# Ten normalizations move from VectorE to GpSimd in the first stage of a decoder kernel

## The chip, the cores and the metric

The kernel runs on one core of a Trainium2 chip. The time is that of one execution on the device in microseconds (us); less is better. In all that follows PE is TensorE (matmuls and transposes), DVE is VectorE, ACT is ScalarE, POOL is GpSimd, and SP is the engine whose queue issues the DMAs.

## What is computed

The reference is a decoder of two layers, all float32, on x of shape (8, 128, 512) and a context of the same shape. After each of six blocks stands the sum with the block's input and a normalization over the last axis:

```python
def _layernorm(x, axis=-1, eps=1e-05):
    m = jnp.mean(x, axis=axis, keepdims=True)
    v = jnp.var(x, axis=axis, keepdims=True)
    return (x - m) / jnp.sqrt(v + eps)
...
x = _layernorm(x + _L0_attn_ref(x, ...))            # causal attention, 32 heads of 16
x = _layernorm(x + _L0_xattn_ref(x, ctx, ctx))      # autocorrelation: FFT, top 9 lags, softmax, shifted sums
x = _layernorm(x + _L0_ffn_ref(x, ...))             # 28 experts of rank 8, the best 2, beside a base matrix
x = _layernorm(x + _L1_attn_ref(x, ...))            # attention with ALiBi
x = _layernorm(x + _L1_xattn_ref(x, ctx, ...))      # attention to the context and itself
x = _layernorm(x + _L1_ffn_ref(x, ...))             # low-rank heads, weighted by a softmax
```

The change concerns the first two of these six normalizations.

## The kernel before

**Tiling.** Each of the 8 batch elements is one block of 128 tokens and so one tile of 128 partitions by 512 features. The program names them by block: x_in_b is the input of block b, x_a0_b the result after the first attention, x_c0_b that after the autocorrelation, x_f0_b after the experts. The profile leaves the numbers out, so x_a and x_c are these tiles (x_a also the ones of the second layer's attention).

**A normalization** is made by two helpers. `add_norm` adds the block's result, which lies in PSUM, to the old x on DVE (L103). `moments` then runs bn_stats (L91), bn_aggr (L93) and the addition of eps (L95) on DVE, which leaves the mean in the tile mv; POOL raises variance plus eps to the power −0.5 (L97), which gives the scale rs. Last, one tensor_scalar over 128x512 subtracts the mean and multiplies by the scale, in place (L107); before the change it runs on DVE. With the argument `later`, everything after the sum is put on a list (`late`) that `catch_up` works off in the next step.

**The first stage** has 16 steps: 4 pairs of blocks by 4 groups of 8 heads. In a step, `Heads16` makes scores in PSUM (L165), adds the mask (L369) and takes the maxima (L182) on DVE; ACT takes the exponentials (L194); a step later `turn` transposes them on PE (L225), with copies out of PSUM on DVE and ACT (L226) under the tile name pT_a, and takes the reciprocal of the sums (L215, rc_a), which POOL spreads over the features (L218, rb_a) for PE to transpose (L233, pr_a); after that `out` multiplies by the values (L244, L250; the result is scaled at L258, oT). Beside it, `queries_keys` prepares the next step (kbd on DVE, L358). The output projection of block b (po, L86) runs in the steps f = 1 and 2 of the next pair; its `add_norm` defers the normalization by a step.

**The autocorrelation** of a pair of blocks is cut into pieces, which the loop places into later steps (pairs 0 and 1) or after it (2 and 3): `spectra` multiplies the normalized x_a and the context with a table of waves on PE (L395: pa from x_a, pb from the context) and forms products (ACT's xa, L401; DVE's L405 and L407; POOL's L406 and L408); `correlate` (pc, L417; ACT's co, L422); `chosen` finds the best lags on DVE (L432 to L446) with help of POOL (L440, L447) and ACT; `shifted` (pvf L457, pw L461, ACT's wf L466, DVE's vw L469 and L471, POOL's L470 and L472); `done` makes poc (L86) and the `add_norm` into x_c. The experts' first reader of x_c transposes it (pt_xTf, L129).

**Order.** Each engine works off its own queue in order. A scheduler in the framework fixes these orders when the program is built, from the order of the calls and its own estimates; `issue_after` pins some of them. PSUM tiles come from two pools, four single banks and two pairs of banks. The scores, pT_a's transposes and pa, pb, pc, pvf and pw share the two pairs, so a matmul into a pair waits for whoever reads the pair's last content.

The stage on which the change bears lies between about 73 and 213 us of the span.

Of the kernel before, what the change touches and what calls it, by code (L numbers as in the profile page):

```python
# [13 lines left out]
ALU = mybir.AluOpType  # L14
# [4 lines left out]
B, S, D = 8, 128, 512  # L19
# [24 lines left out]
def decoder(ctx: ExitStack, tc: tile.TileContext, a: dict, out: bass.AP):  # L44
    nc = tc.nc
# [11 lines left out]
    def bank(name):  # L57
        return ps1.tile([P, 512], F32, tag="ps1", name=name)
# [24 lines left out]
    def mm_acc(ps, pairs):  # L83
        n = len(pairs)
        for i, (l, r) in enumerate(pairs):
            nc.tensor.matmul(ps, lhsT=l, rhs=r, start=(i == 0), stop=(i == n - 1))  # L86

    def moments(src, name):

        st = sm.tile([P, 6], F32, tag="bnst", name=f"st_{name}")  # L90
        nc.vector.bn_stats(st, src)  # L91
        mv = sm.tile([P, 2], F32, tag="bnmv", name=f"mv_{name}")
        nc.vector.bn_aggr(mv, st)  # L93
        ve = sm.tile([P, 1], F32, tag="ve", name=f"ve_{name}")
        moments.done = nc.vector.tensor_scalar(ve, mv[:, 1:2], EPS, None, ALU.add)  # L95
        rs = sm.tile([P, 1], F32, tag="rs", name=f"rs_{name}")
        nc.gpsimd.tensor_tensor(rs, ve, neghalf, ALU.pow)  # L97
        return mv[:, 0:1], rs

    def add_norm(x_old, ps, name, later=None):  # L100

        r = xp.tile([P, D], F32, tag="x", name=f"x_{name}")
        nc.vector.tensor_tensor(r, ps, x_old, ALU.add)  # L103

        def normalized():
            mean, rs = moments(r, name)
            return nc.vector.tensor_scalar(r, r, mean, rs, ALU.subtract, ALU.mult)  # L107

        if later is None:
            add_norm.done = normalized()  # L110
        else:
            later.append(normalized)
        return r

    late = []
# [162 lines left out]
    xs = [None] * B  # L278
# [92 lines left out]
    def projection(b, oT):  # L371
        po = bank(f"po0_{b}")
        mm_acc(po, [(oT[:, b % 2, c, :], wo[:, c, :]) for c in range(NC)])
        nc.gpsimd.tensor_tensor(xs[b], xs[b], bqkv[:, 1, :], ALU.add)
        xs[b] = add_norm(xs[b], po, f"a0_{b}", late)


    def swapped(t):
# [3 lines left out]
    class Correlated:  # L382
# [92 lines left out]
        def done(self, h):  # L475
            b = self.bs[h]
            po = bank(f"poc_{b}")
            mm_acc(po, [(dft[:, T_J + i * P : T_J + (i + 1) * P], self.ri[h][i]) for i in range(2)])
            xs[b] = add_norm(xs[b], po, f"c0_{b}")

        def pieces(self):

# [30 lines left out]
    for n, (p, f) in enumerate(steps):  # L513
# [23 lines left out]
        if 0 < f < 3 and p:  # L537
            projection(2 * p - 3 + f, oTs[p - 1])
# [15 lines left out]
    for j in range(2):  # L554
        projection(B - 2 + j, oTs[NP - 1])
# [56 lines left out]
    def shared_expert(b, xT, hs):  # L612
        po = bank(f"pof0_{b}")
        for c in range(NC):
            shared_expert.done = nc.tensor.matmul(po, lhsT=xT[:, c, :], rhs=wbase[:, c, :], start=(c == 0), stop=False)  # L615
        return hs, po
# [6 lines left out]
    def chosen_experts(b, hT, po, later=None):  # L623
        for j in range(2):
            chosen_experts.done = nc.tensor.matmul(
                po, lhsT=hT[:, j, :], rhs=wlb[:, j, :], start=False, stop=(j == 1)
            )
        xs[b] = add_norm(xs[b], po, f"f0_{b}", later)
# [104 lines left out]
    hs, po = shared_expert(0, *routes[0])  # L733
# [110 lines left out]
    for b in range(B):  # L844
# [3 lines left out]
        for f in (0, 2):  # L848
# [27 lines left out]
            now.divide(0, moments.done if f == 0 and b + 1 < B else None)  # L876
            now.exps(1)
            half = projection(b - 1, oT_before) if f == 2 and b else iter((0, 0))
            next(half)
            if b + 1 < B:  # L880
# [26 lines left out]
    with stage("x1b", 2, side="right") as ap, stage("f1", 2, side="right") as fp:  # L907
# [146 lines left out]
        def turned_heads(b, ls):  # L1054
            pt = bank(f"pt_lT_{b}")
            nc.tensor.transpose(pt[:, :P], ls.rearrange("p h r -> p (h r)"), ident)
            lT = fp.tile([P, P], F32, tag="lT", name=f"lT_{b}")

            nc.scalar.mul(lT, pt[:, :P], H1 * 32.0 / R1)
            return lT  # L1060

        def low_sum(b, lT):
            po = bank(f"pof1_{b}")
            nc.tensor.matmul(po, lhsT=lT, rhs=wb, start=True, stop=True)
            return po
# [12 lines left out]
        def low_scores(b):  # L1078
            scores_low[b] = scored(b, tokens_low.pop(b))

        def low_turn(b):
            turned_lows[b] = turned_heads(b, scores_low.pop(b))
# [87 lines left out]
        po = projection(B - 1, oTs_x.pop(B - 1), {3: [lambda: low_scores(B - 2)], 8: [lambda: low_turn(B - 2)]})  # L1170

        def summed(name, po, x_old):
            r = xp.tile([P, D], F32, tag="x", name=f"x_{name}")
            added = nc.vector.tensor_tensor(r, po, x_old, ALU.add)
            return r, added
# [5 lines left out]
        r, _ = summed("x1_last", po, xs[B - 1])  # L1181
        norm = moments(r, "x1_last")
        po = low_sum(B - 2, turned_lows[B - 2])
# [11 lines left out]
        r, _ = summed(f"f1_{B - 1}", low_sum(B - 1, turned_heads(B - 1, ls)), x_last)  # L1195
# [144 lines left out]
```

## Time and profile before

| | us |
|---|---|
| median of 3 runs | 883.65 |
| lowest and highest | 882.28 and 884.38 |
| the profiled execution | 884.56 |
| its span, first to last instruction | 882.8 |
| busy in the span: PE, DVE, ACT, POOL | 854.3, 565.3, 369.5, 190.3 |
| mean granted TensorE clock | 0.992 |

All rows shown below come from the one profiled execution. Its span is 1.8 us shorter than its own time. Matmuls are pipelined and their ends are modelled, so a busy PE is one that has a matmul under way and not one at its peak. Where a row ends with a bracket, it gives the idle time of the engine before the instruction and what ended it; a row of a group has the count, the busy time and the mean duration in ns; a row with three numbers and slashes has the shortest, median and longest duration in ns.

### The profile page before, as it was taken

How to read it: one execution, taken by the hardware profiler on the slowest of the kernel's cores; microseconds unless marked ns; L12 is line 12 of the kernel's file. 1: busy time of each engine (PE TensorE's matmuls, PEld its weight loads, DVE VectorE, ACT ScalarE, POOL GpSimd, SP SyncE). 2: the span in 40 equal slices, each digit the busy share in tenths (PEclk: the TensorE clock that was granted, in tenths of full speed). 3: DMA queues.
4: the chain of work that ended last, by engine and by line, in shares of the span. 5: the costliest groups of instructions: out<-in, count | busy, mean ns of one | idle time of the engine just before them, and what ended most of it. 6: DMA issues, size and time to landing. Idle time of an engine off the chain costs nothing.

```text
span 882.8 us, 16963 instructions
## 1 busy us (share of the span) xinstructions
PE 854.3 (97%) x6454; PEld 525.1 (59%) x6454; DVE 565.3 (64%) x1329; ACT 369.5 (42%) x1534; POOL 190.3 (22%) x267
## 2 busy tenths in 40 slices
PE   9999999999899999999999999999999999999996
PEld 5766655655445555555555687758475846576442
DVE  3756787786868657888888612725363545467653
ACT  3787465565222216666666603213122322224310
POOL 2500232232333224555555300000000000000000
PEclk9999999999999999999999999999999999999998
DMA  9700000130300002000003020332113211313330
GB/s 329 303 2 25 2 13 13 49 104 6 144 12 24 1 0 72 26 1 2 2 2 144 26 73 1 73 90 46 41 35 93 44 46 38 81 42 80 86 88 36
DMA packets 30066, 50.68 MB, mean 57 GB/s; under 512 B 5536, under 2 KB 22048, under 8 KB 28192
## 3 DMA queue, kind: packets, MB, share of 16 engines
q1 hardware_dynamic: 27424, 47.49, 18.1%
q10 hardware_dynamic: 2560, 2.10, 1.1%
q8 instruction: 51, 0.84, 0.4%
q14 instruction: 31, 0.25, 0.1%
HBM read 30.69 MB, written 2.10 MB: 37 GB/s over the span
## 4 chain that ended last, share of the span: by engine, by line
PE 63%; DVE 21%; ACT 11%; issue 2%; POOL 2%; DMA 1%; SPq 1%; ACTq 0%; POOLq 0%; DVEq 0%
PE pqx L86 9%; PE pox L991 8%; ACT e_a L194 8%; PE pkx L86 4%; PE pvx L86 4%; PE s_x L929 4%; PE o_x L974 4%; PE pq L86 3%; PE pk L86 3%; DVE e_a L715 3%; PE pv L86 3%; DVE m_a L182 2%; PE pof L615 2%; PE pt_a L225 2%; PE s_a L165 2%
## 5 line engine op out<-in xcount | busy, mean ns | idle before, releaser
L194 ACT ACTIVATE e_a<-e_a,m_a 128x128 f32<-128x128 f32 (+1 forms) x512 | 184.8, 364 | 94.3 <-DVE m_a L182 94.3
L950 ACT ACTIVATE e_x<-s_x,m_x 128x256 f32<-128x256 f32 x128 | 58.7, 484 | 139.3 <-DVE m_x L940 130.9
L194 ACT ACTIVATION_READ_ACCUMULATOR e_a<-e_a,m_a 128x1 f32 x512 | 97.0, 189 | 0.0
L991 PE MATMUL pox<-w_X_o,oTx 128*128 128x512 f32 x192 | 84.9, 596 | 0.7 <-DVE oTx L980 0.6
L86 PE MATMUL pqx<-xTx,w_X_q 128*128 128x256 f32 x384 | 84.9, 380 | 0.0
L86 PEld LDWEIGHTS pqx<-xTx,w_X_q 128*128 128x128 f32 x384 | 72.5, 190 | 11.4 <-issue 1.8
L939 DVE TENSOR_REDUCE m_x<-s_x 128x4 f32<-128x1024 f32 x32 | 37.6, 1218 | 41.1 <-PE s_x L929 41.1
L991 PEld LDWEIGHTS pox<-w_X_o,oTx 128*128 128x128 f32 x192 | 35.7, 190 | 46.0 <-issue 44.3
L182 DVE TENSOR_REDUCE m_a<-e_a 128x4 f32<-128x512 f32 (+1 forms) x128 | 62.7, 543 | 0.0
L97 POOL TENSOR_TENSOR rs_x<-ve_x,neghalf 128x1 f32<-128x1 f32 x7 | 3.9, 550 | 268.6 <-DVE ve_x L95 249.6
L208 POOL TENSOR_TENSOR e_a<-e_a,rc_a 128x512 f32<-128x512 f32 x64 | 52.7, 847 | 17.1 <-DVE rc_a L205 16.5
L225 PE MATMUL pt_a<-ident,e_a 128*128 128x128 f32 x384 | 48.6, 274 | 4.5 <-DVE e_a L369 3.9
L225 PEld LDWEIGHTS pt_a<-ident,e_a 128*128 128x128 f32 x384 | 43.5, 140 | 12.3 <-DVE e_a L369 4.9
L929 PE MATMUL s_x<-kTx,qTx 32*128 32x256 f32 x768 | 50.0, 385 | 0.7 <-ACT e_x L950 0.7
L929 PEld LDWEIGHTS s_x<-kTx,qTx 32*128 32x128 f32 x768 | 39.0, 184 | 16.8 <-issue 11.7
L974 PE MATMUL o_x<-pT_x,vx 128*32 128x512 f32 x384 | 43.7, 595 | 1.8 <-issue 0.6
L958 DVE STREAM_TRANSPOSE e_x<-e_x 128x1024 f32<-128x1024 f32 x32 | 39.7, 1241 | 0.8
L957 DVE TENSOR_SCALAR e_x<-e_x,rc_x 128x256 f32<-128x256 f32 x128 | 36.3, 347 | 3.9 <-DVE rc_x L954 2.6
L103 DVE TENSOR_TENSOR x_x<-pox,x_a 128x512 f32<-128x512 f32 x7 | 4.8, 686 | 52.5 <-PE pox L991 52.5
L165 PEld LDWEIGHTS s_a<-kbd,qT 32*64 32x64 f32 x1024 | 20.7, 131 | 28.4 <-issue 12.7
L835 ACT COPY qTx<-pqx 128x512 f32<-128x512 f32 x24 | 14.1, 594 | 55.5 <-PE pqx L86 55.2
L165 PE MATMUL s_a<-kbd,qT 32*64 32x256 f32 (+1 forms) x1024 | 33.2, 335 | 2.1 <-DVE pT_a L226 1.2
(223 smaller groups left out, 1618.0 us busy)
## 6 DMA issues: line engine op xcount, KB each, us to landing
pT_x<-e_x SPq DMA_DIRECT2D x224, 64.0 KB, 2.0
w_X_q<-in_X_q SPq DMA_DIRECT2D x3, 1024.0 KB, 4.9
w_X_o<-in_X_o SPq DMA_DIRECT2D x3, 1024.0 KB, 4.8
w_L_Wv<-in_L_Wv SPq DMA_DIRECT2D x2, 1024.0 KB, 6.7
w_L_Wo<-in_L_Wo SPq DMA_DIRECT2D x2, 1024.0 KB, 7.6
x_in<-in_x SPq DMA_DIRECT2D x8, 256.0 KB, 7.5
ct<-in_ctx SPq DMA_DIRECT2D x8, 256.0 KB, 2.8
cT<-in_ctxT SPq DMA_DIRECT2D x4, 512.0 KB, 3.8
```

The lines of the kernel that those rows point to most:

```text
L86: nc.tensor.matmul(ps, lhsT=l, rhs=r, start=(i == 0), stop=(i == n - 1))
L165: nc.tensor.matmul(s[r // 2][64 * u : 64 * u + 64, r % 2, cols], lhsT=qT[rows, 64 - 64 * part : P - 64 * part], rhs=kbd[rows, :, :keys], s ...
L182: self.scored = nc.vector.tensor_reduce(self.m[:, part, rs, :], self.by_heads(part)[:, rs], AX.X, ALU.max, negate=True)
L194: nc.scalar.activation(e[:, r, x, :], e[:, r, x, :], AF.Exp, bias=self.m[:, part, r, x : x + 1], accum_out=self.su[:, part, r, x : x + 1],)
L208: nc.gpsimd.tensor_tensor(e, e, bc(self.rc[:, part, rs, :].unsqueeze(3), list(e.shape)), ALU.mult)
L225: nc.tensor.transpose(pt[:, r, cols], self.e[:, 2 * i + r, cols], ident)
L929: nc.tensor.matmul(sc[g // 2][:, g % 2, u * 256 : (u + 1) * 256], lhsT=qT[rows, (h0 + u) * NS + n, :], rhs=kT[rows, n], start=(n == 0), st ...
L939: nc.vector.tensor_reduce(m, self.s[i], AX.X, ALU.max, negate=True)
L950: nc.scalar.activation(self.e[:, :, j, :], self.s[half][:, i, :].rearrange("p (a k) -> p a k", k=32), AF.Exp, bias=self.m[:, j : j + 1], s ...
L958: nc.vector.transpose(self.e[:, :, js, :], self.e[:, :, js, :])
L974: nc.tensor.matmul(po[32 * g : 32 * g + 32, :], lhsT=v[:, s, g * XD + 32 * n : g * XD + 32 * n + 32], rhs=pT[:, s].rearrange("p i h x -> p ...
L991: nc.tensor.matmul(po, lhsT=oT[:, n, h * P : (h + 1) * P], rhs=w, start=(i == 0), stop=(i == NX - 1))
```

## The change

`add_norm` takes the engine of the final tensor_scalar as an argument. For the first attention, blocks 0 to 5 pass GpSimd, and blocks 6 and 7 VectorE as before; for the autocorrelation, blocks 0 to 3 pass GpSimd, and 4 to 7 VectorE. These are ten instructions. Sums, moments and scales stay where they were. In the changed file the lines from 101 on have numbers that are higher by one.

```diff
-    def add_norm(x_old, ps, name, later=None):
+    def add_norm(x_old, ps, name, later=None, engine=nc.vector):
+
 
         r = xp.tile([P, D], F32, tag="x", name=f"x_{name}")
         nc.vector.tensor_tensor(r, ps, x_old, ALU.add)
 
         def normalized():
             mean, rs = moments(r, name)
-            return nc.vector.tensor_scalar(r, r, mean, rs, ALU.subtract, ALU.mult)
+            return engine.tensor_scalar(r, r, mean, rs, ALU.subtract, ALU.mult)
...
-        xs[b] = add_norm(xs[b], po, f"a0_{b}", late)
+        xs[b] = add_norm(xs[b], po, f"a0_{b}", late, nc.gpsimd if b < B - 2 else nc.vector)
...
-            xs[b] = add_norm(xs[b], po, f"c0_{b}")
+            xs[b] = add_norm(xs[b], po, f"c0_{b}", engine=nc.gpsimd if b < B // 2 else nc.vector)
```

## Prediction

> **What bounds the kernel now.** I read the page first: busy times and the chain.
>
> ```profile
> PE 854.3 (97%) x6454; PEld 525.1 (59%) x6454; DVE 565.3 (64%) x1329; ACT 369.5 (42%) x1534; POOL 190.3 (22%) x267
> PE 63%; DVE 21%; ACT 11%; issue 2%; POOL 2%; DMA 1%; SPq 1%; ACTq 0%; POOLq 0%; DVEq 0%
> ```
>
> PE is hardly ever without a matmul, so shorter DVE work pays only where PE stands still and the wait ends on DVE. The ten instructions that move lie between 73 and 213 us. So I then asked for PE's waits from 60 to 225 us, which answers in six lines:
>
> ```profile
> PE pt_a L225 <- DVE e_a L369: 3.9, 2, 2.0
> PE pa L395 <- DVE pT_a L226: 0.6, 1, 0.6
> PE o_a L244 <- DVE ve_a L95: 0.4, 1, 0.4
> PE pt_a L225 <- ACT e_a L194: 0.4, 1, 0.4
> PE pvf L457 <- ACT pT_a L226: 0.3, 1, 0.3
> PE s_a L165 <- DVE vw L471: 0.2, 1, 0.2
> ```
>
> Columns: total us, times, longest. All PE idling in the stage is 5.8 us. The 3.9 us are two waits behind the top-k work (110 to 112 and 174 to 176 us); no moved instruction runs near them. Only the second line has one on its path, as the chain from 72 to 92 us shows (start, us, what):
>
> ```profile
> 83.22 0.15 DVE ve_a L95
> 83.37 0.66 DVE kbd L358
> 84.03 0.01 issue
> 84.05 0.55 DVE x_a L107
> 84.59 0.88 DVE pT_a L226
> 85.47 0.04 issue
> 85.51 1.94 PE pa L395 x8
> ```
>
> x_a here is token block 1. The normalization stands on DVE ahead of the copy that frees the PSUM pair which pa wants; PE's previous matmuls ended at 84.87.
>
> **Removed from DVE.** Ten L107 instructions (x_a of blocks 0 to 5, x_c of 0 to 3). L107's view gives:
>
> ```profile
> L107 DVE TENSOR_SCALAR x_a<-x_a,mv_a,rs_a x16: 540/546/1418, 73.6 to 513.2; 128x512 f32<-128x512 f32 x16
> ```
>
> Ten times 0.546 is 5.5 us of DVE. In the built order of the changed program PE, ACT and SP keep their order, DVE loses the ten (and one bn_aggr passes an oT multiply), and on POOL each stands directly behind the L97 of its norm. What follows each on DVE decides:
>
> - x_a 0 (73.64): pT_a comes 0.5 earlier, then DVE idles 2.76 us for ACT's exps, with PE unbroken. Zero.
> - x_a 1 (84.05): pT_a starts at 84.03, pa at about 84.95 instead of 85.51. Gain 0.55. It holds downstream: s_a at 91.87 needs the PSUM pairs that DVE's L407 frees at 91.64; L405 ahead of it waits for ACT's xa (to 89.7, ACT busy throughout) and can move forward about 0.2, so s_a arrives at 91.3 and finds its second pair free at about 91.5, which it wants 0.2 later. I book 0.5.
> - x_a 2, 3, 4 (129.81, 145.96, 192.38): the next but one on DVE is L103 x_c, which waits 0.9 us for PE's poc. Zero each.
> - x_c 0, 2 (134.63, 197.21): DVE then idles 2.04 us for ACT's wf. Zero.
> - x_c 1 (151.50): DVE waits 0.88 us for rs_c, then goes on with L405, for which pb ends at 151.8; the following v waits 1.14 us for PE. Zero.
> - x_a 5, x_c 3 (209.25, 211.99): ACT's exps end the wait of pt_a at 211.71. Only pa at 212.19, which the trace shows 0.17 us behind DVE's pT_a on the weight load, can come earlier: 0 to 0.17; I take 0.1.
>
> Cover for the zeros is PE's own stream; were it gone, they would be worth at most 8 × 0.55 = 4.4 us.
>
> **Added on POOL.** No row shows a 128x512 tensor_scalar there. The nearest:
>
> ```profile
> L440 POOL TENSOR_TENSOR ex<-co,top 128x512 f32<-128x512 f32 x8 | 8.4, 1049 | 21.3 <-DVE top L432 21.2
> L408 POOL TENSOR_TENSOR pr<-pr 128x512 f32<-128x512 f32 x4 | 5.1, 1275 | 3.7 <-DVE mv_f L93 3.7
> L270 POOL MEMSET vd<- 128x512 f32 x6 | 3.4, 572 | 0.0
> ```
>
> A memset (writes only) 0.57, two full inputs 1.28, one full and one broadcast input 1.05. The last is nearest in shape: I take t = 1.05, ends 0.57 and 1.28. In all 10.5 us more POOL, which is at 22%.
>
> [...]
>
> Readers of the results. x_a 1 is the only tight one: rs ends at 84.00, t puts it ready at 85.1; pa reads block 0 first (two calls each of about 0.43 × 2 us, block 1 from 84.95 + 0.86 = 85.8). Slack 0.7, so it holds to t = 1.75. x_a 3 is ready at 147.0, read from 149.0. x_a 5 at 210.3, read from 213. x_c 0 to 3 are read by the transposes at 207.5, 210.1 and after 239; for 2 and 3 that is over 25 us.
>
> Queued behind each on POOL: after x_a 0, 1, 3 POOL idled 4.6 us, after x_a 2 and 4 4.3 us ahead of rs_c: absorbed. Behind x_c 0 and x_c 2 stands rb_a with only 0.3 us to spare, so it ends about 0.5 to 0.7 later; its reader, PE's pr_a, comes 8 us later or more. Behind x_c 1 comes L406, 1.8 us away. Behind x_a 5 and x_c 3: rs_c 3 (before at 211.08) starts by 210.7, x_c 3 ends near 212.3, rb_a near 212.7 (before 213.24; PE wants it at 213.36). Zero.
>
> **A shared port.** One of the DVE rows shows a clash: x_a at 224.28 took 1.42 us while POOL ran memsets until 226.2; that one (block 6) stays. The work beside the ten moved ones on DVE reads PSUM (pT_a, L103, L405) or is a bn_stats; the pT_a row is 906 to 958 ns in all 32 cases. I cost contention at zero, with up to 0.4 us at x_c 3 where a reciprocal (L215) may wait.
>
> [...]
>
> **Sum.** −0.5 − 0.1 = −0.6 us. The profiled execution took 884.56 (span 882.8 and 1.8 around it), 0.9 above the median 883.65: 884.0 for such an execution, **883.05** for the median. As bounds of the mechanism: −0.7 to +0.4 (gain lost and the reciprocal's wait).
>
> **What can blur it.** PE's granted clock falls in places after an idle stretch: it is 0.79 over 112 to 120 us.
>
> ```profile
> 113.88 2.08 PE L86 MATMUL po<-w_L_Wo,oT 128*128 128x512 f32 x2
> 115.75 2.54 PE L457 MATMUL pvf<-ct,dft 128*128 128x512 f32 x4
> ...
> 177.35 1.12 PE L86 MATMUL po<-w_L_Wo,oT 128*128 128x512 f32 x2
> 178.80 1.98 PE L457 MATMUL pvf<-ct,dft 128*128 128x512 f32 x4 [0.33 <-ACT pT_a L226]
> ```
>
> The same work 64 us later, behind an equal 1.96 us of idling, runs at full clock: one slow stretch costs (2.08 − 1.12) + (2.54 − 1.98) = 1.5 us, and it does not always come. The three times before span 2.1 us, so a median can shift by one.
>
> [...]
>
> **Rivals.**
> 1. *No change in kind (chance 0.50).* The sum above; 881.9 to 885.4.
> 2. *Faster (0.31).* The 0.6 and one slow stretch fewer: 883.65 − 0.6 − 1.5 = 881.5. For it: 0.55 us less idling and earlier phases in a stage with three idle stretches of 2 us. Or part of the covered 4.4 us becomes real, where PE's continuous busy time hides waits (s_a at 122.51 took 1.86 for 0.91). Against: those waits end on vw and ACT.
> 3. *Slower (0.19).* POOL's tensor_scalar with two per-partition operands is slow. From t = 1.75 pa waits for x_a 1. From t = 1.55 rb_a 3_3 (209.25 + t + 0.55 + t + 0.40, wanted at 213.3) holds pr_a, at 2 us for each us of t. At t = 2.5: 0.75 + 1.9 − 0.6 = +2.0, so 885.7. For it: L97's single column takes 0.55 us, far more than its one element explains. Against: every full-width row of POOL is under 1.3.
> 4. *The move does nothing on DVE* (the waits it removes were PE's anyway): 883.65, within case 1.
>
> **Chances.** 0.2% is 1.77 us, about what a measurement of this kernel can tell from no change. Faster by more needs −1.2 beyond my sum, slower +2.4. 0.31, 0.50 and 0.19. Range: from 883.65 − 0.7 − 1.5 − 0.5 (one slow stretch fewer and one of the eight covered instructions turned real) = 881.0 to 883.65 + 0.4 + 1.5 (one slow stretch more) = 885.5.
>
> **What would show it.** Right: pa's wait of 0.64 gone, x_a and x_c on POOL at about 1.05, DVE's busy time down by some 5.5, rb_a never ending a PE wait, PE's two waits of 2.0 unchanged. Wrong: a PE wait that ends on x_a or rb_a; POOL's L107 over 1.55; a gain over 1.2 at PE's unchanged clock.

## The result and the profile after

The changed kernel took 886.44 us (median of 8 runs, 884.56 to 887.34) against 883.91 for the kernel before in the same comparison (8 runs, 882.28 to 884.90): a ratio of 1.0027, interval 1.0016 to 1.0038. A second comparison, shown below as e12, gave 1.0029 (1.0019 to 1.0039). So the change costs 2.2 to 2.5 us; the forecast was a gain of 0.6. The profiled execution took 887.34 with a span of 885.6, 2.8 longer than the span before.

Line numbers are those of the changed file, one higher than before from 101 on. The page's busy times and the shares of the chain:

```profile
PE 855.7 (97%) x6454; PEld 526.1 (59%) x6454; DVE 560.7 (63%) x1319; ACT 369.5 (42%) x1534; POOL 210.1 (24%) x277
...
PE 61%; DVE 21%; ACT 12%; POOL 2%; issue 2%; DMA 1%; ACTq 0%; POOLq 0%; DVEq 0%; SPq 0%
```

DVE lost 4.6 us. That is less than ten times 0.546, because the rows of neighbouring instructions overlap in the profile (before, the row behind x_a 0 begins 0.47 us after it) and because one other instruction took 0.47 longer (the last section). POOL gained 19.8, where the forecast booked 10.5. POOL's rows, grouped by form, say why:

```profile
L108 POOL TENSOR_SCALAR x_a<-x_a,mv_a,rs_a 128x512 f32<-128x512 f32 x6 | 12.5, 2080 | 0.6
...
L108 POOL TENSOR_SCALAR x_c<-x_c,mv_c,rs_c 128x512 f32<-128x512 f32 x4 | 8.3, 2077 | 0.4
```

One of them takes 2.08 us, 3.8 times its 0.546 on DVE. PE's waits from 60 to 225 us (total us, times, longest) show where that reaches the engine that sets the end:

```profile
PE pt_a L226 <- DVE e_a L370: 3.9, 2, 2.0
PE pr_a L234 <- POOL rb_a L219: 1.0, 1, 1.0
PE o_a L245 <- DVE ve_a L95: 0.4, 1, 0.4
...
PE pa L396 <- POOL x_a L108: 0.2, 1, 0.2
```

The two long waits behind the top-k work are what they were. pa's wait of 0.64 on DVE's copy is gone, as the change meant it. Two new waits end on POOL, and both are of this change.

**The first place, at 84 us.** PE's timeline in the changed kernel:

```profile
84.40 1.02 PE L86 MATMUL pv<-w_L_Wv,xT 128*128 128x512 f32 x2
85.57 1.07 PE L396 MATMUL pa<-x_a,dft 128*64 128x512 f32 x2
86.88 1.50 PE L396 MATMUL pa<-x_a,dft 128*64 128x512 f32 x5 [0.24 <-POOL x_a L108]
...
90.46 1.12 PE L86 MATMUL pv<-w_L_Wv,xT 128*128 128x512 f32 x2
```

Before, pa started at 85.51, with no wait inside it, between these two rows:

```profile
83.85 1.02 PE L86 MATMUL pv<-w_L_Wv,xT 128*128 128x512 f32 x2
...
89.10 2.84 PE L86 MATMUL pv<-w_L_Wv,xT 128*128 128x512 f32 x6
```

From pv to pa 1.66 became 1.17 us, the gain of 0.5 that was forecast. From pa to pv 3.59 became 4.89, a loss of 1.3. Net +0.81, and this still holds behind the next matmuls (from pv to the first o_a 9.67 us, 8.85 before). The bracket shows only 0.24 of idling; the rest of the loss is hidden in PE's busy time, and the experiments explain it.

**The second place, at 213 us.** POOL's timeline, and PE's beside it:

```profile
210.21 0.56 POOL L97 TENSOR_TENSOR rs_a<-ve_a,neghalf 128x1 f32<-128x1 f32 x1 [5.04 <-DVE ve_a L95]
210.88 2.08 POOL L108 TENSOR_SCALAR x_a<-x_a,mv_a,rs_a 128x512 f32<-128x512 f32 x1
212.93 0.56 POOL L97 TENSOR_TENSOR rs_c<-ve_c,neghalf 128x1 f32<-128x1 f32 x1
213.60 2.08 POOL L108 TENSOR_SCALAR x_c<-x_c,mv_c,rs_c 128x512 f32<-128x512 f32 x1
215.62 0.40 POOL L219 COPY rb_a<-rc_a 128x256 f32<-128x256 f32 x1
```

```profile
214.74 0.33 PE L226 MATMUL pt_a<-ident,e_a 128*128 128x128 f32 x1
216.07 0.44 PE L234 MATMUL pr_a<-ident,rb_a 128*128 128x128 f32 x2 [1.01 <-POOL rb_a L219]
```

Before the change PE's two rows were these:

```profile
213.19 0.33 PE L225 MATMUL pt_a<-ident,e_a 128*128 128x128 f32 x1
213.36 0.38 PE L233 MATMUL pr_a<-ident,rb_a 128*128 128x128 f32 x2
```

POOL works without a gap from the scale of block 5 to rb_a; both long instructions stand ahead of a copy of 0.40 that PE wants. From the last pt_a to pr_a it was 0.17 us before (213.19 to 213.36) and is 1.33 here: +1.16.

0.81 and 1.16 make 2.0 of the 2.2 to 2.5 us. The two spans differ by 2.8: beside these 2.0, the start took 0.5 longer and x_a of block 6 another 0.5 (the last section for both), while the program's last two matmuls took 1.12 where they took 1.89, at a granted clock of 0.97 from 860 to 882 us where it was 0.84; some 0.5 us more is spread over the rest.

### The profile page after: what moved, and what is told of

Its sections match the earlier page's. It is cut to its first block, busy times and chain, and to the rows that moved or that the text cites. A ratio compares the mean times of both kernels' runs of the same rounds, so it can differ in the third digit from the quotient of the medians.

```text
span 885.6 us, 16973 instructions
## 1 busy us (share of the span) xinstructions
PE 855.7 (97%) x6454; PEld 526.1 (59%) x6454; DVE 560.7 (63%) x1319; ACT 369.5 (42%) x1534; POOL 210.1 (24%) x277
## 4 chain that ended last, share of the span: by engine, by line
PE 61%; DVE 21%; ACT 12%; POOL 2%; issue 2%; DMA 1%; ACTq 0%; POOLq 0%; DVEq 0%; SPq 0%
PE pqx L86 9%; ACT e_a L195 8%; PE pox L992 8%; PE pkx L86 4%; PE pvx L86 4%; PE s_x L930 4%; PE o_x L975 4%; PE pq L86 3%; DVE e_a L716 3%; DVE m_a L183 3%; PE pk L86 3%; PE pv L86 2%; PE pof L616 2%; PE pt_a L226 1%; PE po L86 1%
## 5 line engine op out<-in xcount | busy, mean ns | idle before, releaser
L97 POOL TENSOR_TENSOR rs_x<-ve_x,neghalf 128x1 f32<-128x1 f32 x7 | 3.8, 548 | 268.9 <-DVE ve_x L95 249.9
```

## The experiments

Two theories. **Late results:** a GpSimd instruction of 2.08 us costs only where somebody wants its result, or a result queued behind it, at once; that is at block 1 and at block 5 with x_c 3. **Toll:** each moved instruction costs some 0.25 us (the 2.5 of the change over ten), by a clash with VectorE or by later work on GpSimd. Each timed kernel is compared with the kernel before in runs on the same chip; differences are of medians. The brackets hold the ratio to the kernel before and its 95% interval; the ratio is estimated by itself and can differ from that of the medians by half a microsecond and more.

**Taking them back.** e1 puts block 1 of the attention back on VectorE, e2 block 3 of the autocorrelation, e3 both. Their edits are the conditions in the two calls, in e3:

```diff
-        xs[b] = add_norm(xs[b], po, f"a0_{b}", late, nc.gpsimd if b < B - 2 else nc.vector)
+        xs[b] = add_norm(xs[b], po, f"a0_{b}", late, nc.gpsimd if b in (0, 2, 3, 4, 5) else nc.vector)
...
-            xs[b] = add_norm(xs[b], po, f"c0_{b}", engine=nc.gpsimd if b < B // 2 else nc.vector)
+            xs[b] = add_norm(xs[b], po, f"c0_{b}", engine=nc.gpsimd if b < 3 else nc.vector)
```

> Undoes one of the ten: x_a of block 1 is normalized on DVE again, nine stay on POOL. Theory (two late results: x_a 1 for pa, worth +0.8 us net, and rb_a behind x_a 5 and x_c 3, worth +1.2; another 0.5 in a DVE row of 1.89 us at x_a 6): pa waits 0.6 us for DVE's pT_a as before the change, rb_a still ends a PE wait of 1.0; the time is 0.8 below the changed kernel, +1.2 to +1.7 over the kernel before. Rival (a toll on each moved instruction, by semaphores or the shared port, some 0.25 us each): only 0.25 below the changed kernel, +2.2 over before.

> Undoes another one: x_c of block 3 is normalized on DVE again, nine stay on POOL, x_a 5 among them. Theory: POOL's queue ahead of rb_a then holds only x_a 5 and rs_c 3, so rb_a ends about 0.9 us ahead of PE's want and PE's wait of 1.0 on it is gone, while pa's wait for x_a 1 stays; +0.8 to +1.3 over the kernel before. Rival (toll on each): +2.2 over before.

> Undoes these two together; eight of ten stay on POOL, at 2.08 us each. Theory: both PE waits gone, 0.0 to +0.5 over the kernel before (the 0.5 if the DVE row at x_a 6 takes 1.89 instead of 1.42 us). Rival (toll on each): +2.0 over before.

Measured: e1 +0.7 us (1.0010, 1.0000 to 1.0019), e2 +1.4 (1.0024, 1.0015 to 1.0033), e3 +1.6 (1.0012, 1.0003 to 1.0021). e1's median lies below what was expected, with an interval that reaches it; its waits are the expected ones: pa's on x_a is replaced by one of 0.7 on pT_a (0.6 before the change), and the 1.0 on rb_a stays. e2 and e3 missed: rb_a's wait is gone in both, but the loss is not. DVE's timeline in e3 shows where it went:

```profile
212.66 0.55 DVE L108 TENSOR_SCALAR x_c<-x_c,mv_c,rs_c 128x512 f32<-128x512 f32 x1 [1.22 <-POOL rs_c L97]
213.12 0.95 DVE L227 COPY pT_a<-pt_a 128x768 f32<-128x768 f32 x1
```

rs_c still stands behind block 5's 2.08 us on POOL. x_c 3, back on DVE ahead of the copy pT_a, now waits for it and holds that copy, and PE's pa waits 0.74 us for the copy. From the first pt_a behind ACT's exponentials to pa's second part it is 3.10 us (212.40 to 215.50), 1.96 before (211.71 to 213.67): the loss of 1.1 has another victim; its source, block 5, had stayed.

**Shorter instructions.** In e4 block 1 and all the others stay on GpSimd, but the ten only subtract the mean; the kernel leaves out their multiplication by the scale:

```diff
+            if engine is nc.gpsimd:
+                return engine.tensor_scalar(r, r, mean, None, ALU.subtract)
```

> The ten on POOL only subtract the mean; the multiplication by the scale is left out. Order and number of instructions stay. Theory (the length is the cause, and each of the two operations is a pass of its own): POOL's rows take about 1.05 us; rb_a is never late, x_a 1 is ready within 0.2 us of pa's start; between -0.5 and +0.3 against the kernel before. Rival (toll on each, whatever its length): +2 over before. If the rows stay at 2 us, the second operation is free and the time stays at +2.5.

Measured: −0.2 us (0.9999, 0.9990 to 1.0007). The row, 1.57 us where 1.05 was expected:

```profile
L109 POOL TENSOR_SCALAR x_a<-x_a,mv_a 128x512 f32<-128x512 f32 x6 | 9.4, 1572 | 26.0 <-DVE mv_a L93 26.0
```

It also starts earlier, since it does not wait for the scale: x_a 0 begins 1.2 us behind the start of its st_a (71.8 to 73.0), where it was 2.0 in the change (72.24 to 74.26). No wait on rb_a or x_a is left. Ten moved instructions that are shorter and earlier cost nothing, which speaks against a toll.

**Parts of the change alone.** e5 keeps seven on GpSimd (attention 0, 2, 3, 4; autocorrelation 0, 1, 2), e6 only block 1, e7 only block 5 and x_c 3; again only the two conditions differ.

> Block 1 and block 5 of the attention and block 3 of the autocorrelation are on VectorE again, seven normalizations stay on GpSimd. Theory (only late results cost: x_a 1 at 84 us, and at 210 us whatever stands on GpSimd behind x_a 5): none of pa <- x_a, pr_a <- rb_a, or pa <- pT_a at 0.7 us in the 210 us region is left beyond what the kernel before had; time 0.0 against the kernel before, between -0.6 and +0.6. Rival (a toll of some 0.25 us on each moved instruction, by the shared port or by GpSimd's later work): 7 x 0.25 = +1.7 us. The bystander, the memset clash of block 6 (1.42 or 1.89 us), can add 0.5 to either.

> Only block 1 of the attention is on GpSimd. Theory: pa starts some 0.5 us earlier and its second half then waits for x_a 1 (0.2 us shown, pa's five last matmuls at half the rate), +0.8 us against the kernel before (0.5 to 1.2); the waits at 210 us as in the kernel before. Rival (toll on each): +0.25 us.

> Only block 5 of the attention and block 3 of the autocorrelation are on GpSimd. Theory: pr_a waits about 1.0 us for rb_a 3_3, as with all ten moved, and pa at 85 us as in the kernel before with its wait of 0.6 on pT_a: +1.2 us (0.8 to 1.5). Rival (toll on each): +0.5 us.

Measured: e5 +0.5 us (1.0005, 0.9996 to 1.0013), e6 +0.3 (1.0004, 0.9995 to 1.0012), e7 +0.8 (1.0011, 1.0002 to 1.0019). Seven instructions at a toll would have cost 1.7, a ratio of 1.0019, outside e5's interval; a toll under 0.16 each is not excluded by it. e6's timeline has the first place exactly as the change has it (pa 84.83, the third matmul 86.14, pv 89.72), and e7's waits the 1.0 on rb_a. Their medians lie below the 0.81 and 1.16 of the traces, which are inside the intervals. e6's interval holds 0 as well, so the price of block 1 rests on the traces, and not on its time alone.

**The change once more.**

> The change itself once more, with 5 rounds. If its parts add up (medians: block 1 alone +0.3, block 5 and x_c 3 alone +0.8, the seven others +0.5): +1.6 us against the kernel before, 1.0 to 2.2; if the first result of +2.5 holds, up to 0.9 us belongs to none of the parts.

Measured: +2.2 us (1.0029, 1.0019 to 1.0039; the interval is 1.7 to 3.4 us), so nearer to the first result than to the 1.6 of the parts. Each of the three parts has an interval of about 0.8 us on either side, so whether something belongs to none of them stays open.

**Prices on GpSimd.** e9 gives six of the places with slack other forms.

```diff
+        "a0_0": lambda r, m, s: nc.gpsimd.tensor_scalar(r, r, m, None, ALU.subtract),
+        "a0_2": lambda r, m, s: nc.gpsimd.tensor_scalar(r, r, s, None, ALU.mult),
+        "a0_3": lambda r, m, s: nc.gpsimd.tensor_scalar(r, r, 0.5, None, ALU.mult),
+        "a0_4": lambda r, m, s: nc.gpsimd.tensor_scalar(r, r, 0.25, 0.5, ALU.subtract, ALU.mult),
+        "c0_0": lambda r, m, s: nc.gpsimd.tensor_tensor(r, r, bc(s, [P, D]), ALU.mult),
+        "c0_2": lambda r, m, s: nc.gpsimd.tensor_copy(r, r),
```

> A price list on GpSimd at places that have slack: at x_a 0 one subtraction by a per-partition column, at x_a 2 one multiplication by a column, at x_a 3 one multiplication by a constant, at x_a 4 a subtraction and a multiplication by constants, at x_c 0 a tensor_tensor with the scale spread by a stride of zero, at x_c 2 a plain copy, at x_a 5 and x_c 1 the change's form with two columns; the other normalizations as before. Parts of these six normalizations are left out. If the columns make it slow, constants stay under 1.1 us; if it is the number of operations, all with one operation take 1.57 and both with two 2.08. The tensor_tensor 1.05 as in L440's row, the copy between the memset's 0.57 and 1.05.

POOL's groups by form (busy, mean ns):

```profile
L120 POOL TENSOR_SCALAR x_c<-x_c,mv_c,rs_c 128x512 f32<-128x512 f32 x1 | 2.1, 2080 | 0.1
...
L104 POOL TENSOR_SCALAR x_a<-x_a 128x512 f32<-128x512 f32 x1 | 1.9, 1926 | 3.7 <-DVE st_a L91 3.7
L102 POOL TENSOR_SCALAR x_a<-x_a,rs_a 128x512 f32<-128x512 f32 x1 | 1.6, 1580 | 0.1
L101 POOL TENSOR_SCALAR x_a<-x_a,mv_a 128x512 f32<-128x512 f32 x1 | 1.6, 1573 | 4.7 <-DVE mv_a L93 4.7
L103 POOL TENSOR_SCALAR x_a<-x_a 128x512 f32<-128x512 f32 x1 | 1.5, 1505 | 3.7 <-DVE st_a L91 3.7
L105 POOL TENSOR_TENSOR x_c<-x_c,rs_c 128x512 f32<-128x512 f32 x1 | 1.0, 1040 | 0.1
L106 POOL COPY x_c<-x_c 128x512 f32<-128x512 f32 x1 | 0.6, 611 | 2.5 <-DVE st_c L91 2.5
```

Neither expectation holds alone. The columns cost little (0.07 us for one, 2.08 − 1.93 = 0.15 for two), the second operation 0.42 to 0.51. What costs most is the form: a tensor_scalar with one operation by a constant takes 1.50, a tensor_tensor that multiplies by the same scale, spread by a stride of zero, 1.04.

The number of full inputs does not order these prices: in e9 one full input takes 1.50 to 2.08 us as a tensor_scalar and 0.61 as a copy, and two full inputs take 1.27 to 1.28 as a tensor_tensor (pr and vw).

**Why the first place costs 0.8.** The forecast gave x_a 1 a slack of 0.7 us, since pa begins with block 0. e13 changes only L395's order on the kernel before, e16 times it, e14 and e15 put the same order on the change and on e6:

```diff
-                for i in range(2):
-                    for h, b in enumerate(self.bs):
+                for h, b in enumerate(self.bs):
+                    for i in range(2):
```

> All normalizations on VectorE as before; only the order of L395's matmuls is changed: both of the first block of a pair, then both of the second, where the kernel before alternates between the blocks. If matmuls into different 64-column halves run beside each other only when they alternate (the reading that makes block 1 wanted as soon as pa starts), pa's eight records take some 3.5 us where they took 1.9, and the same for pb: about 1.8 us more for each of the eight tiles, up to +14 us in all, less where PE had idled. If each matmul takes 0.22 us by itself, whatever stands beside it (the prediction's slack of 0.7 us for x_a 1 failed for another reason), pa stays at 1.9 us and the time within 0.5 us.

> The change with all ten on GpSimd, and L395's matmuls in order of the blocks. In the traces these matmuls' records start two by two, 0.43 us a pair, in either order; in the change the first one is alone (85.57 and 86.05), since the next in the queue waits for x_a 1, and every later pair is shifted by one, so that the last is alone as well: the two ahead save nothing. If this is the cause, in order of the blocks both of block 0 run before the wait, block 1's start at 86.9 as before with only their own half left: pv some 0.9 us earlier relative to pa's start than in the change, and the time +1.3 us against the kernel before instead of +2.2 to +2.5 (the wait of 1.0 us for rb_a stays). If the loss at 84 us has another cause, +2.2 as for the change.

> Only block 1 of the attention on GpSimd, and L395's matmuls in order of the blocks. By the shifted pairs: pa starts 0.5 us earlier, block 1's matmuls wait some 0.4 us longer than they otherwise would: 0.0 against the kernel before (-0.3 to +0.3). If the loss has another cause, +0.3 to +0.8 as with block 1 alone.

> All normalizations on VectorE, L395's matmuls in order of the blocks, now timed: 0.0 against the kernel before (-0.3 to +0.3) if the pairs form in either order, as the trace of its first run has it.

Measured: e14 +3.3 us (1.0028, 1.0016 to 1.0041), e15 +1.0 (1.0010, 0.9997 to 1.0022), e16 −0.2 (0.9996, 0.9987 to 1.0005). e13's pa stays at 1.94 us, so the first reading failed, that the pairs need the alternating order. The gain of 0.9 expected of e14 failed too, though its wait on x_a is gone from the list. The weight loads of e14 show why, and end e13's second reading as well (0.22 us for each by itself). Each call for pa and pb shows as two passes, each with a weight load of its own (in e13's view of L395 32 loads and 32 matmuls for pa's 16 calls):

```profile
84.94 0.19 PEld L396 LDWEIGHTS pa<-x_a,dft 128*64 128x64 f32 x2 [0.98 <-DVE pT_a L227]
85.42 0.14 PEld L396 LDWEIGHTS pa<-x_a,dft 128*64 128x64 f32 x1 [0.29 <-issue]
85.85 0.14 PEld L396 LDWEIGHTS pa<-x_a,dft 128*64 128x64 f32 x1 [0.29 <-issue]
86.25 0.19 PEld L396 LDWEIGHTS pa<-x_a,dft 128*64 128x64 f32 x2 [0.27 <-POOL x_a L108]
86.33 0.13 PEld L396 LDWEIGHTS pb<-ct,dft 128*64 128x64 f32 x1
86.71 0.14 PEld L396 LDWEIGHTS pb<-ct,dft 128*64 128x64 f32 x1 [0.24 <-issue]
86.73 0.14 PEld L396 LDWEIGHTS pa<-x_a,dft 128*64 128x64 f32 x1
```

and those of e16, where everything is ready:

```profile
86.00 0.20 PEld L395 LDWEIGHTS pa<-x_a,dft 128*64 128x64 f32 x4 [1.46 <-DVE pT_a L226]
86.48 0.15 PEld L395 LDWEIGHTS pa<-x_a,dft 128*64 128x64 f32 x2 [0.28 <-issue]
86.91 0.15 PEld L395 LDWEIGHTS pa<-x_a,dft 128*64 128x64 f32 x2 [0.28 <-issue]
```

In e14 block 0's passes go one at a time every 0.43 us while block 1 is missing; then block 1's run beside pb's first. Ready, they go two by two. So two passes of one half came 0.43 us apart (e14's pb at 86.70, 87.13 and 87.56), and two of different halves side by side (its pa at 86.73, 87.16 and 87.59). The two blocks write different halves of the 128 output partitions (64h to 64h + 63), and each half was here a lane that took one pass in 0.43 us. Block 1's lane has eight passes, four of pa and four of pb, in a row: 8 × 0.43 = 3.4 us, and whatever block 0 does ahead shortens nothing. From the first matmul of block 1 to pv it is 3.59 us in the kernel before (85.51 to 89.10), 3.58 in the change (86.88 to 90.46), 3.58 in e6 (86.14 to 89.72) and 3.58 in e14 (86.25, its weight load, to 89.83), in either order. So x_a 1 is wanted when pa can start.

In e14 and e16 the calls stand in the kernel in this order: pa's of block 0, pa's of block 1, then pb's in the same way. In e14 pb's first matmul starts at 86.70 and pa's last at 87.59; in e16 they start two by two although two of one half stand next to each other. So PE's matmuls did not all start in the order of their calls; whether the built program or PE itself set them so, no run shows. That an engine works off its queue in order, as the section on order says of each, is seen here on POOL (in the change rb_a starts at 215.62 behind x_c, 1.47 us after its rc_a, 213.90 and 0.25 long) and on DVE (in e3 pT_a starts at 213.12, behind an x_c that waits 1.22).

**An order on VectorE alone.** Half of the change's idea is that x_a 1 need not stand ahead of the copy that frees pa's PSUM pair. e8 gets that on VectorE: its order there is made ve_a, pT_a, x_a 1, kbd. e10 is e8 with the seven of e5 on GpSimd, e11 is e8 once more.

```diff
+        if n == begun:
+            with tc.issue_after(prev.copied.ins):
+                scaled = add_norm.scaled()
+            with tc.issue_after(scaled.ins):
+                queries_keys.keys()
```

> All sixteen normalizations are on VectorE as before; in the step at 83 us VectorE's order is made ve_a, pT_a, x_a 1, kbd, where the kernel before has ve_a, kbd, x_a 1, pT_a. By the theory that pa's first matmul needs only pT_a's pair free and block 0, and that x_a 1 is ready 0.55 us later on VectorE, pa starts 0.7 earlier and its second half waits about 0.2 for x_a 1: -0.5 us against the kernel before (-0.2 to -0.7). If kbd, now 0.6 us later, becomes what s_a waits for, the gain is lost: 0.0.

> VectorE's order of the version with kbd behind x_a 1, and the seven harmless normalizations (blocks 0, 2, 3, 4 of the attention, 0, 1, 2 of the autocorrelation) on GpSimd. If VectorE's time at these seven places is covered by PE, moving them adds nothing: the same as the version with kbd behind alone, -0.5 to -1.0 us against the kernel before. Rival (their 3.8 us of VectorE become real once pa no longer waits): -1.5 us or more.

> The version with kbd behind x_a 1 once more, beside the two others: -0.5 to -1.2 us against the kernel before if its first result was no chance; 0.0 if it was.

Measured: e8 −0.9 us (0.9986, 0.9977 to 0.9996), e10 −0.5 (0.9993, 0.9984 to 1.0002), e11 −0.1 (0.9994, 0.9986 to 1.0003). e8's timeline:

```profile
84.51 1.02 PE L86 MATMUL pv<-w_L_Wv,xT 128*128 128x512 f32 x2
85.47 1.94 PE L403 MATMUL pa<-x_a,dft 128*64 128x512 f32 x8
87.23 1.89 PE L403 MATMUL pb<-ct,dft 128*64 128x512 f32 x8
89.05 2.84 PE L86 MATMUL pv<-w_L_Wv,xT 128*128 128x512 f32 x6
91.82 1.34 PE L169 MATMUL s_a<-kbd,qT 32*64 32x256 f32 x32
```

pa starts without a wait, and x_a 1 comes in time, which the expectation had 0.2 late. From pv to pv it is 4.54 us, 5.25 before, in the timeline of e11 too (84.30 to 88.84). But most of these 0.7 us are lost again at s_a, which took 0.91 before:

```profile
91.87 0.91 PE L165 MATMUL s_a<-kbd,qT 32*64 32x256 f32 x32
```

s_a needs the PSUM pair that DVE's second product with pb frees. In e8 the first of these products waits 0.64 us for ACT's xa, and the second ends at 92.14, 7.63 us after pv's start where it was 7.79; of s_a's 32 matmuls 4 started before 92.0, and the last ended at 93.16, 1.02 us behind that product. From pv to the first o_a behind s_a it is 8.58 us in e8 and e11, 8.85 before. So 0.3 of the 0.7 us are left in both traces; in the times only e8's interval excludes no change. Against the changed kernel all three are faster by over 2 us. e10 speaks for VectorE's time at the seven places being covered: moving them on top gains nothing.

## Why the prediction was wrong

The step that failed is the term **"Added on POOL"**: t was taken as 1.05 with ends of 0.57 and 1.28, and is 2.08. The rows behind it were tensor_tensors and a memset; a tensor_scalar of this shape had another price there, 2.08 us, and no row of like operation could tell it. L97's 0.55 us for a single element a partition, named in rival 3, was the better warning.

- **What follows from t** was worked out in rival 3, and that rival came true in its mechanism: a PE wait on rb_a and one on x_a. That its number, +2.0 at t = 2.5, lies near the measured one is luck, since at t = 2.08 its formula gives +0.8 (the next point). The place at 213 us: at 2 us for each us of t over 1.55 it gives 1.06; the trace has 1.16.
- **Readers of the results:** the second error. x_a 1's slack of 0.7 came from two calls of block 0 ahead of it at 0.43 × 2 each; with the two blocks in separate lanes there is none. The chain's row in the prediction showed it: pa's eight passes took 1.94 us, and one after the other they would take 8 × 0.43 = 3.4. x_a 1 would have to end by pa's start, 85.57 − 84.75 = 0.8 us after its own, so the taken 1.05 would already have given back 0.2 of the 0.5, and the threshold of 1.75 was wrong by 0.9. By rival 3's formula the change would cost 0.33 + 1.06 − 0.6 = +0.8; the 0.9 missed at block 1, the 0.1 missed at rb_a and the 0.1 booked as a gain at 212 us make it 1.9, the traces' 2.0.
- **Removed from DVE:** right as to pa's wait, which is gone, and "zero each" held: e5 and e10 show no gain from the seven others. But the 0.5 do not hold downstream as booked. In e4, where no result is late, pv to pv is 0.49 us shorter than before, and from pv to the first o_a 0.21 are left (8.64 us, 8.85 before), since s_a takes 1.18 us for 0.91. So even a short t would have left a gain of about 0.2.
- **Queued behind each on POOL:** right behind the other eight, even at 2.08 us: nothing there reached PE. Wrong for rb_a 3_3, through t alone.
- **A shared port** as a cost of the move: none was seen, and no run shows such a port. The copies pT_a on DVE took 0.933 us in the mean, 0.935 before, and the reciprocal at x_c 3 0.25, 0.24 before: the 0.4 us that the upper bound has for it were not there.
- **The chances:** the forecast's 0.50 for no change and 0.19 for slower leaned on "every full-width row of POOL is under 1.3". That was evidence on another operation.
- **The range** ended at 885.5, below the 885.7 that rival 3 itself gave; two losses of about a microsecond at known places were left out above it. The 1.5 us that it books for a slow stretch is too much: from po to pw behind pvf it is 4.25 us in the slow stretch (113.88 to 118.13) and 3.27 in the other (177.35 to 180.62), so 1.0. The working added the lengths of rows that overlap.

## What to carry to other kernels

Where no row shows an operation on the engine it moves to, rows of the same shape are no bound: here they had 0.57 to 1.28 us and the instruction took 2.08, 3.8 times its time on DVE. The forecast has to carry such a case. For each moved instruction find the first reader of its result and of everything queued behind it; seven of ten moves here cost nothing that the times could tell, at four times the duration, and three make up the 2.0 us that the traces show. And where a tile is filled in halves that run beside each other, as pa was, the half that comes last sets the end (3.58 to 3.59 us from its first matmul to pv, in either order), so the slack of its input is counted from the start of the pair. A gain at one wait is followed to the next ones, which can lie inside rows that look busy: here 0.5 became 0.2.

## What the runs showed of the hardware

- **GpSimd** at 128x512 float32, in e9: copy 0.61 us, tensor_tensor 1.04 to 1.28, tensor_scalar 1.50 with one constant, 1.57 to 1.58 with one column, 1.93 with two constants, 2.08 with two columns; on VectorE the last took 0.546 in the kernel before (median of L107).
- **One VectorE instruction beside memsets.** x_a of block 6, which nobody moved, took 1.42 us in the kernel before and 1.89 in the change:

```profile
227.06 1.89 DVE L108 TENSOR_SCALAR x_a<-x_a,mv_a,rs_a 128x512 f32<-128x512 f32 x1 [0.68 <-POOL rs_a L97]
```

  POOL runs memsets beside it in both. In e13 and e16, with all normalizations on VectorE, it took 1.89 as well; in e3, e5 and e6, 1.42. With 1.42 the last of the memsets takes 0.80 us (the kernel before, e3, e5), with 1.89 it takes 0.53 (the change, e8, e10, e12). The longer one reaches PE, whose wait on ex behind it is 1.3 us and not 0.9. No moved instruction is needed for it, but whether these 0.47 us are part of the cost of the change stays open: both traces of the changed kernel have 1.89, and the kernel before has one trace. e16, with 1.89 and otherwise like the kernel before, measured −0.2 us (−1.1 to +0.4), which speaks against it, by a narrow margin. What decides between the two values stays open.
- **The start.** pk's first matmul came at 7.43 us in the kernel before and at 8.11 in the change, ahead of every moved instruction. pq ahead of it started at 5.29 and 5.63, behind the transfer of xT, and then took 1.97 and 2.64. In e12, the same program, pk began at 7.14. The span of a single trace carries some 0.5 us of this.
- **The slow stretch** of PE's clock came in the change too, at the other of its two places (granted 0.79 over 176 to 184 us and 1.00 over 112 to 120; before, 1.00 and 0.79):

```profile
177.89 2.08 PE L86 MATMUL po<-w_L_Wo,oT 128*128 128x512 f32 x2
179.76 2.54 PE L458 MATMUL pvf<-ct,dft 128*128 128x512 f32 x4
```

  The same two rows at 115.24 and 116.69 took 1.13 and 1.98. Before, it was the other way round, so the two, 1.0 us each, cancel between the profiles.
